# B's product of each scan state: on VectorE in the first attention and the thought, on GpSimd in the second attention's loop

## The chip, the core and the metric

The kernel runs on one core of a Trainium2 chip. The metric is the device time of one launch in microseconds (us); lower is better. A core has TensorE (PE), VectorE (DVE), ScalarE (ACT), GpSimd (POOL) and SyncE (SP), which here only issues DMAs. Each engine works through its own list of instructions in order and waits for the others by semaphores.

## What is computed

A decoder of four layers of three parts each runs on a stream x of 4 x 256 tokens with 256 features; each part adds its output to x and normalizes. The parts that matter are the first three and the next two: an attention with 16 heads (`L0_attn`), a selective scan whose output gates x (`L0_xattn`), a gated block with four recurrent "thought" steps (`L0_ffn`), a second attention (`L1_attn`) and a second selective scan (`L1_xattn`). Both scans read only the context, not x, so each can be computed any time before its gate. The scan, cut to its core:

```python
delta = softplus(dt_proj_w @ dt_lo + dt_proj_b)     # per channel and token
A = -exp(A_log)                                      # 16 states per channel
def step(state, xs):
    d_t, B_t, C_t, u_t = xs
    dA = exp(d_t[..., None] * A)
    state = state * dA + (d_t * u_t)[..., None] * B_t[:, None, :]
    y_t = einsum('ben,bn->be', state, C_t)
    return state, y_t
y = (y + D * u) * silu(z)                            # z is the stream x
```

There are 256 channels, 16 states, 4 batch elements and 256 tokens.

## The kernel before

One program does all twelve parts. Activations stay in on-chip memory; weights are loaded one part ahead. All arithmetic named below is in float32.

**The scans.** Class `Scans` (lines 398 to 531) makes both scans. Its generator `_steps` first makes u, delta and du = delta * u for all tokens (lines 446 to 487), and writes the rows of B and C to DRAM. Then come 4 x 16 = 64 "states", one for each batch element and state number. One state, on tiles of 128 partitions x 512 (two channel halves x 256 tokens), is:

- a DMA on SP's queue that spreads one row of B and one of C over all partitions, tile `bc` (line 513; 256 KB);
- two activations on ACT that make `dA` (line 517), in one of three buffers;
- the product `s = du * B` (line 519), by `K.ptt`, that is on GpSimd. This is "B's product" of the title;
- the scan along time on VectorE, in place in `s` (line 520);
- the product `s = s * C` on VectorE (line 528, by `K.tt`);
- two states later, a matmul with the identity on TensorE that adds `s` into a PSUM bank, tile `ssmps` (line 499, function `add`).

Pools `bc` and `s` have four buffers each (line 403). So a state's DMA waits for the C product of four states before, and B's product waits for the DMA and for TensorE's sum of four states before, whose buffer `s` it overwrites.

**Beside what the states run.** `K.scans.beside(n)` (line 432) takes the next n states out of the generator. The first scan's 64 states go beside the first attention, two for each of its 32 iterations (`run_mqa`, line 378). The second scan's first 24 go into the thought in one burst (`run_thought`, line 748), 8 into the preparation of the second attention (`run_gqa`, line 1030), and 32 into its loop (line 1034).

**An iteration of the first attention** (lines 368 to 384) has, on VectorE: the maxima of the scores (`nm`, line 311), the query product and the two rotated halves from PSUM (`qT`, `ropet`, lines 259 to 261, each reading one operand from PSUM), the reciprocals (`sm`, line 320). GpSimd adds the rotated halves (`qT<-qT,ropet`, line 262, both operands in on-chip memory). ACT makes the exponentials `p`, their scaling, and copies `pT` and `oT` out of PSUM. TensorE makes scores `sc`, transposes, sums `o`, the output projection `acc` and the next queries `ps`. Every eighth iteration ends a batch element: x is updated and normalized twice (`x<-x,mv,rstd`, line 164), with a GpSimd power for `rstd` in the middle (lines 166 to 170), and `gate_pair` (line 534) multiplies the gate on GpSimd.

**A thought step** (lines 708 to 739) is a chain: `rstd` on VectorE and its power on GpSimd, `tT` on VectorE, matmuls, Gelu on ACT, transposes, matmuls, and back to the next step's variance.

The order of the instructions in each engine's list is set by a scheduler when the program is built. It starts from the order of the code above and its own estimates of cost, and the list is then fixed. Helpers have one line each: `K.tt` is line 111 (VectorE), `K.ptt` line 123 (GpSimd), `K.mm` line 132 (TensorE), `K.act` line 126 (ACT).

Of the kernel before, what the change touches and what calls it, by code (L numbers as in the profile page):

```python
# [29 lines left out]
ADD, SUB, MUL, MAX, MIN = ALU.add, ALU.subtract, ALU.mult, ALU.max, ALU.min  # L30

P = 128
B, L, D = 4, 256, 256
NT = B * L // P
DC = D // P
# [5 lines left out]
class Core:  # L41


    def __init__(self, tc, ctx, A, out, first, last):
        self.tc, self.nc, self.A, self.out, self.first, self.last = tc, tc.nc, A, out, first, last
        nc = tc.nc
        const = ctx.enter_context(tc.tile_pool(name="const", bufs=1))
        self.state = ctx.enter_context(tc.tile_pool(name="state", bufs=1))
        self.x = self.state.tile([P, NT, D], F32, name="x")
        self.xT = self.state.tile([P, DC, B * L], F32, name="xT")  # L50

        self.ctxp = self.state.tile([P, B, L + 3], F32, name="ctxp")
        nc.gpsimd.memset(self.ctxp[:, :, 0:3], 0.0)
        xT = A["xT"].rearrange("(c p) t -> p c t", p=P)
        for h in range(2):
            nc.sync.dma_start(out=self.xT[:, :, 512 * h : 512 * h + 512], in_=xT[:, :, 512 * h : 512 * h + 512])

        self.idz = const.tile([P, 2 * P], F32, name="idz")
        nc.gpsimd.memset(self.idz, 0.0)
        make_identity(nc, self.idz[:, 0:P])  # L60
        self.ident = self.idz[:, 0:P]

        self.identb = const.tile([P, P], BF16, name="identb")
        nc.vector.tensor_copy(self.identb, self.ident)
        self.fin = ctx.enter_context(tc.tile_pool(name="fin", bufs=3))
        self.mean = const.tile([P, 3], F32, name="mean")
        self.power = const.tile([P, 2], F32, name="power")
        nc.gpsimd.memset(self.power, -0.5)
        self.ones = const.tile([P, P], F32, name="ones")
        nc.gpsimd.memset(self.ones, 1.0)  # L70
        self.eps = {}
        for v in (1e-6, 1.0):
            self.eps[v] = const.tile([P, 1], F32, name=f"eps{len(self.eps)}")
            nc.gpsimd.memset(self.eps[v], v)
        self._turn = 0
# [130 lines left out]
def again(ap, n):  # L206

    return ap.unsqueeze(1).to_broadcast([ap.shape[0], n, ap.shape[1]])
# [189 lines left out]
class Scans:  # L398
    def __init__(self, K, ctx):
        tc = K.tc  # L400
        self.K = K
        self.one = ctx.enter_context(tc.tile_pool(name="ssm1", bufs=1))
        self.wk = ctx.enter_context(tc.tile_pool(name="ssm2", bufs=4))
        self.ps = ctx.enter_context(tc.tile_pool(name="ssmp", bufs=1, space=PSUM))
        self.dram = ctx.enter_context(tc.tile_pool(name="ssmd", bufs=2, space=bass.MemoryType.DRAM))

        self.dA = [self.one.tile([P, DC, L], F32, name=f"dA{k}") for k in range(3)]
        for t in self.dA:
            K.nc.gpsimd.memset(t[:, :, 0:1], 0.0)
        self.w = {}  # L410
        self.left = iter(())
        self.done = 0

    def load(self, pre):
        K = self.K
# [26 lines left out]
    def _steps(self, pre):  # L442
        K, nc, w, wk = self.K, self.K.nc, self.w[pre], self.wk
        cols = w["cols"]
        N = B * L
        u = self.one.tile([P, DC, N], F32, name="u", bufs=2)
        delta = self.one.tile([P, DC, N], F32, name="delta")
        du = self.one.tile([P, DC, N], F32, name="du")


        taps = []
        for j in range(4):
            t = wk.tile([P, D], F32, name="tap", tag="bc", padded_shape=[P, 2 * L])
            nc.sync.dma_start(out=t, in_=K.A[f"{pre}_cw"][:, j * D : (j + 1) * D].to_broadcast([P, D]))
            K.ptt(t, t, w["in"], MUL)
            taps.append(t)
        for h in range(2):
            for c in range(DC):
                ps = self.bank()
                for j in range(4):  # L460
                    K.mm(ps, taps[j][:, c * P : (c + 1) * P], K.ctxp[:, 2 * h : 2 * h + 2, j : j + L], j == 0, j == 3)
                K.act(u[:, c, 512 * h : 512 * h + 512], ps, AF.Identity, bias=cols[:, c, 0:1])
        K.act(u, u, AF.Silu)
        negA = self.one.tile([P, DC, 16], F32, name="negA")
        K.act(negA, cols[:, :, 2:18], AF.Exp)
        K.ts(negA, negA, -1.0, None, MUL)
        bc = self.dram.tile([2, 16, N], F32, name="bcd")
        for h in range(2):
            s = slice(512 * h, 512 * h + 512)
            xd = wk.tile([P, 512], F32, name="xd", tag="s")  # L470
            ps = self.bank()
            for c in range(DC):
                K.mm(ps[0:40, :], w["xp"][:, c, :], u[:, c, s], c == 0, c == DC - 1)
            nc.scalar.copy(xd[0:40, :], ps[0:40, :])
            for k in range(2):
                nc.sync.dma_start(out=bc[k, :, s], in_=xd[8 + 16 * k : 24 + 16 * k, :])
            for c in range(DC):
                ps = self.bank()
                K.mm(ps, w["dt"][:, c * P : (c + 1) * P], xd[0:8, :])

                K.ts(delta[:, c, s], ps, cols[:, c, 1:2], None, ADD)
                K.act(du[:, c, s], ps, AF.Abs, bias=cols[:, c, 1:2])
        K.act(du, du, AF.Exp, scale=-1.0)
        K.act(du, du, AF.Ln, bias=K.eps[1.0])
        for c in range(DC):
            K.stt(delta[:, c, :], delta[:, c, :], 0.0, du[:, c, :], MAX, ADD)
            K.ptt(du[:, c, :], delta[:, c, :], u[:, c, :], MUL)

        turn = 0
        self.y = u  # L490

        late = []
        bank = {}

        def add(b, n, s):
            if n == 0:
                bank[b] = self.bank()
            y = bank[b]
            K.mm(y, K.ident, s.rearrange("p c l -> p (c l)"), n == 0, n == 15)
            if n == 15:  # L500
                for c in range(DC):
                    v = u[:, c, b * L : (b + 1) * L]
                    K.stt(v, v, cols[:, c, 18:19], y[:, c * L : (c + 1) * L], MUL, ADD)
                self.done += 1

        for b in range(B):
            lo = b * L
            for n in range(16):
                yield
                if len(late) > 1:  # L510
                    add(*late.pop(0))
                t = wk.tile([P, 2, L], F32, name="bc", tag="bc")
                nc.sync.dma_start(out=t, in_=bc[:, n, lo : lo + L].unsqueeze(0).to_broadcast([P, 2, L]))
                dA = self.dA[turn % 3]
                turn += 1
                for c in range(DC):
                    K.act(dA[:, c, 1:L], delta[:, c, lo + 1 : lo + L], AF.Exp, scale=negA[:, c, n : n + 1])
                s = wk.tile([P, DC, L], F32, name="s")
                K.ptt(s, du[:, :, lo : lo + L], again(t[:, 0, :], DC), MUL)
                nc.vector.tensor_tensor_scan(  # L520
                    out=s.rearrange("p c l -> p (c l)"),
                    data0=dA.rearrange("p c l -> p (c l)"),
                    data1=s.rearrange("p c l -> p (c l)"),
                    initial=0.0,
                    op0=MUL,
                    op1=ADD,
                )
                K.tt(s, s, again(t[:, 1, :], DC), MUL)
                late.append((b, n, s))
        for t in late:  # L530
            add(*t)


def gate_pair(K, pool, y, b):

    K.scans.upto(b)
    gate = pool.tile([P, DC, L], F32, name="gate")

    K.act(gate, K.x[:, 2 * b : 2 * b + 2, :], AF.Silu)
    K.ptt(gate, gate, y[:, :, b * L : (b + 1) * L], MUL)  # L540
    for t in range(2):
        ps = K.tp.tile([P, 512], F32, name="ps", tag="tp")
        for c in range(DC):
            K.nc.tensor.transpose(ps[:, c * P : (c + 1) * P], gate[:, c, t * P : (t + 1) * P], K.ident)
        K.add_out(2 * b + t, ps[:, 0:D])
# [436 lines left out]
def run_gqa(K, w, more):  # L982
    nc, tc = K.nc, K.tc
    more()
    with ExitStack() as ctx:
# [22 lines left out]
        for i in range(NT):  # L1008
# [6 lines left out]
            t = [wk.tile([P, 20, 8], F32, name=f"t{k}") for k in range(4)]  # L1015
# [15 lines left out]
        early.close()  # L1031
        if K.fused(3):
            heads16.then = lambda b: gate_pair(K, wk, K.scans.y, b)
        heads16.run(ctx, lambda: K.scans.beside(1))


# [1401 lines left out]
```

## Time and profile before

| | |
|---|---|
| runs shown | 2521.07, 2504.77, 2520.05 us; median 2520.05 |
| the profiled execution | 2505.99 us; span 2504.2 us, so 1.8 us lie around the span |
| granted TensorE clock, mean | 0.939 of full speed |
| busy: PE, DVE, ACT, POOL | 2277.2, 1460.8, 802.4, 530.6 us |
| first scan of a state begins, 64th ends | 88.6 us, 382.8 us |
| the thought's 24 states | 467.4 to 540 us |
| the preparation's 8 states | 565 to 612 us |
| the loop's 32 states | 612 to 773 us |

In the profile each group of instructions has the line that issued it, the engine, the operation, out<-in with the tiles' names, shapes and the count; behind the bar come the busy time in us, the mean of one in ns, and the engine's idle time just before these instructions with what ended it. In the timeline each row has the start and the time taken, both in us; "x2" after a row says that two alike followed each other and were merged.

### The profile page before, as it was taken

How to read it: one execution, taken by the hardware profiler on the slowest of the kernel's cores; microseconds unless marked ns; L12 is line 12 of the kernel's file. 1: busy time of each engine (PE TensorE's matmuls, PEld its weight loads, DVE VectorE, ACT ScalarE, POOL GpSimd, SP SyncE). 2: the span in 40 equal slices, each digit the busy share in tenths (PEclk: the TensorE clock that was granted, in tenths of full speed). 3: DMA queues.
4: the chain of work that ended last, by engine and by line, in shares of the span. 5: the costliest groups of instructions: out<-in, count | busy, mean ns of one | idle time of the engine just before them, and what ended most of it. 6: DMA issues, size and time to landing. Idle time of an engine off the chain costs nothing. (4 is left out here: it accounts for less than half of the span.)

```text
span 2504.2 us, 28859 instructions
## 1 busy us (share of the span) xinstructions
PE 2277.2 (91%) x10624; PEld 1526.3 (61%) x10624; DVE 1460.8 (58%) x2824; ACT 802.4 (32%) x1781; POOL 530.6 (21%) x617
## 2 busy tenths in 40 slices
PE   8798988648996999989999999999999989799997
PEld 5466654224443565545888888888776544476774
DVE  3798984588875412182356454444555667774556
ACT  3566663422442111153111111111122244343434
POOL 2544543663332222210001100011110002100001
PEclk9899999677987999999999999999988899999999
DMA  5221221122223254230123111211100002100000
GB/s 197 60 60 45 57 54 40 41 61 42 52 46 109 88 158 130 66 112 29 45 66 110 48 58 45 71 46 47 46 22 1 20 18 70 40 1 1 1 1 17
DMA packets 132836, 138.99 MB, mean 56 GB/s; under 512 B 13876, under 2 KB 120726, under 8 KB 130904
## 3 DMA queue, kind: packets, MB, share of 16 engines
q1 hardware_dynamic: 132696, 137.16, 19.1%
q8 instruction: 84, 1.38, 0.2%
q14 instruction: 56, 0.46, 0.1%
HBM read 134.27 MB, written 2.85 MB: 55 GB/s over the span
## 5 line engine op out<-in xcount | busy, mean ns | idle before, releaser
L132 PE MATMUL ps<-xw,xcT 128*128 128x256 f32 (+1 forms) x2304 | 519.0, 382 | 0.3 <-ACT YT L126 0.3
L132 PEld LDWEIGHTS ps<-xw,xcT 128*128 128x128 f32 x2304 | 430.7, 190 | 64.2 <-issue 1.9
L132 PE MATMUL sc<-kT,qT 32*128 32x256 f32 (+2 forms) x1024 | 240.7, 412 | 11.1 <-DVE qn L129 10.7
L520 DVE TENSOR_TENSOR_SCAN s<-dA,s 128x512 f32<-128x512 f32 x128 | 210.3, 1666 | 35.6 <-POOL s L123 35.4
L123 POOL TENSOR_TENSOR s<-du,bc 128x512 f32<-128x512 f32 x128 | 178.9, 1410 | 231.0 <-PE ssmps L132 191.1
L132 PEld LDWEIGHTS sc<-kT,qT 128*128 128x128 f32 (+1 forms) x1024 | 152.9, 206 | 92.3 <-issue 57.8
L132 PE MATMUL ssmps<-s,idz 128*128 128x512 f32 x256 | 147.1, 683 | 33.6 <-DVE s L111 33.5
L111 DVE TENSOR_TENSOR xp<-ps,xb 128x256 f32<-128x256 f32 x96 | 40.4, 421 | 227.0 <-PE ps L132 224.8
L126 ACT ACTIVATE dA<-delta,negA 128x255 f32<-128x255 f32 x256 | 117.7, 501 | 160.5 <-DVE s L520 160.3
L126 ACT ACTIVATE p<-sc,nm 128x256 f32<-128x256 f32 (+1 forms) x256 | 112.1, 445 | 109.5 <-DVE nm L129 103.7
L111 DVE TENSOR_TENSOR hT<-u,a 128x512 f32<-128x512 f32 x48 | 33.2, 691 | 186.1 <-PE u L132 186.1
L132 PE MATMUL o<-pT,vt 128*128 128x256 f32 (+1 forms) x352 | 121.1, 467 | 21.9 <-ACT pT L332 21.5
L123 POOL TENSOR_TENSOR xp<-xp,rn 128x128 f32<-128x128 f32 x96 | 35.2, 402 | 476.9 <-DVE rn L1406 476.9
L169 POOL TENSOR_SCALAR rstd<-mv 128x2 f32<-128x2 f32 x48 | 12.2, 255 | 551.3 <-DVE mv L161 541.4
L126 ACT ACTIVATE sq<-xp 128x1024 f32<-128x1024 f32 x24 | 25.4, 1057 | 314.3 <-DVE xp L111 314.2
L129 DVE TENSOR_REDUCE qn<-sc 128x2 f32<-128x480 f32 (+1 forms) x192 | 87.2, 506 | 43.6 <-PE sc L132 42.9
L129 DVE TENSOR_REDUCE nm<-sc 128x2 f32<-128x512 f32 (+1 forms) x128 | 77.2, 613 | 49.8 <-PE sc L132 49.2
L126 ACT ACTIVATE e<-sT 128x512 f32<-128x512 f32 x128 | 70.1, 591 | 108.3 <-PE sT L132 107.8
L1474 DVE TENSOR_TENSOR_SCAN dec<-xT,idz 128x256 f32<-128x256 f32 (+1 forms) x192 | 89.8, 537 | 25.0 <-DMA xT<-ad 25.0
L111 DVE TENSOR_TENSOR s<-s,bc 128x512 f32<-128x512 f32 x128 | 103.6, 829 | 1.1
L123 POOL TENSOR_TENSOR hT<-hT,sel 128x512 f32<-128x512 f32 x48 | 60.7, 1268 | 202.1 <-DVE hT L111 102.6
L132 PE MATMUL sT<-q,kT 32*128 32x256 f32 (+1 forms) x384 | 96.4, 502 | 1.7 <-ACT e L126 1.5
(503 smaller groups left out, 4067.1 us busy)
## 6 DMA issues: line engine op xcount, KB each, us to landing
bc<-bcd SPq DMA_DIRECT2D x128, 256.0 KB, 4.6
xw<-in_l2a_xw_dram SPq DMA_DIRECT2D x24, 768.0 KB, 4.9
xT<-ad SPq DMA_DIRECT2D x12, 1024.0 KB, 4.5
wj<-in_l1f_gate_dram SPq DMA_DIRECT2D x48, 128.0 KB, 2.6
wj<-in_l1f_up_dram SPq DMA_DIRECT2D x48, 128.0 KB, 3.1
wj<-in_l1f_down_dram SPq DMA_DIRECT2D x48, 128.0 KB, 3.5
sel<-cwd SPq DMA_DIRECT2D x32, 192.0 KB, 3.0
sel<-cwd SPq DMA_DIRECT2D x32, 128.0 KB, 3.5
```

Of the source, the lines that this page charges most:

```text
L111: self.nc.vector.tensor_tensor(out=out, in0=a, in1=b, op=op)
L123: self.nc.gpsimd.tensor_tensor(out=out, in0=a, in1=b, op=op)
L126: self.nc.scalar.activation(out, in_, func, **kw)
L129: self.nc.vector.tensor_reduce(out=out, in_=in_, axis=AX.X, op=op, **kw)
L132: self.nc.tensor.matmul(out, lhsT=lhsT, rhs=rhs, start=start, stop=stop)
L169: self.nc.gpsimd.tensor_scalar(out=out, in0=in_, scalar1=add, scalar2=None, op0=ADD)
L520: nc.vector.tensor_tensor_scan(out=s.rearrange("p c l -> p (c l)"), data0=dA.rearrange("p c l -> p (c l)"), data1=s.rearrange("p c l -> p ...
L1474: nc.vector.tensor_tensor_scan(out=dec[:, k, h, :], data0=ap[:, h, at(bb, k, j) : at(bb, k, 2)], data1=K.idz[:, 0 : (2 - j) * P], initial=0.0,
```

## The change

B's product is issued on VectorE (`K.tt`) unless a flag `apart` is set. The flag starts as false and is set when the preparation of the second attention is over, ahead of its loop. So the 64 states of the first attention, 24 of the thought and 8 of the preparation get B's product on VectorE, and the 32 of the loop keep it on GpSimd. Nothing else is edited.

```diff
@@ class Scans, __init__
         self.done = 0
+        self.apart = False
@@ Scans._steps
-                K.ptt(s, du[:, :, lo : lo + L], again(t[:, 0, :], DC), MUL)
+                (K.ptt if self.apart else K.tt)(s, du[:, :, lo : lo + L], again(t[:, 0, :], DC), MUL)
@@ run_gqa
             heads16.then = lambda b: gate_pair(K, wk, K.scans.y, b)
+        K.scans.apart = True
         heads16.run(ctx, lambda: K.scans.beside(1))
```

In the lists of the changed program, the typical iteration of the first attention reads on VectorE: two maxima, `qT`, two `ropet`, the reciprocals, two B products, two scans, two C products. SP's list is the same as before, and all lists agree again from the first states of the second attention's loop on. In the burst of the thought, each B product stands one state ahead of the scan that uses it.

## The prediction

> **What bounds the kernel now.** I read the page's busy digits first: where do the scans lie (slices of 62.6 us, so the first 13), and who is full there?
>
> ```profile
> PE   8798988648996999989999999999999989799997
> DVE  3798984588875412182356454444555667774556
> POOL 2544543663332222210001100011110002100001
> PEclk9899999677987999999999999999988899999999
> ```
>
> VectorE is at 8 to 9 tenths in slices 2 to 5 and 8 to 10 but far from it later. Only there can the change matter; behind 775 us VectorE is busy for 883 of 1729 us, and the lists are unchanged. Next, the stretches (columns after the length: PE, PEld, DVE, ACT, POOL busy, clock, DMA share, GB/s): first attention, thought, preparation.
>
> ```profile
> 84.60:385.00 300.40, 260.50 (x1070) 178.06 (x1070) 264.00 (x338) 186.74 (x532) 152.23 (x109) 0.94 0.23 55
> 465.00:540.50 75.50, 47.39 (x200) 20.86 (x201) 67.31 (x64) 32.45 (x65) 48.85 (x32) 0.82 0.35 77
> 565.00:612.00 47.00, 39.80 (x155) 22.12 (x156) 41.89 (x86) 12.44 (x35) 20.67 (x39) 0.83 0.22 45
> ```
>
> VectorE is the fullest engine in all three (88, 89 and 89%); in the first attention PE is level with it (87%). In its steady part PE is even the tighter one: over the two iterations from 214.67 to 232.37 PE is busy 17.70 of 17.70 us, VectorE 16.33. But what is in VectorE's busy time? Groups of 84.6 to 385 us:
>
> ```profile
> L520 DVE TENSOR_TENSOR_SCAN s<-dA,s 128x512 f32<-128x512 f32 x64 | 116.7, 1857 | 10.7 <-POOL s L123 10.5
> L111 DVE TENSOR_TENSOR s<-s,bc 128x512 f32<-128x512 f32 x64 | 49.1, 798 | 0.2
> L117 DVE TENSOR_SCALAR x<-x,mv,rstd 128x256 f32<-128x256 f32 x12 | 12.0, 1041 | 5.0 <-POOL rstd L123 5.0
> L123 POOL TENSOR_TENSOR s<-du,bc 128x512 f32<-128x512 f32 x64 | 85.4, 1353 | 99.5 <-PE ssmps L132 87.3 <-DMA bc<-bcd 8.6 <-PE ps L330 3.4
> L123 POOL TENSOR_TENSOR qT<-qT,ropet 128x512 f32<-128x512 f32 x24 | 49.7, 2070 | 15.6 <-DVE ropet L111 15.6
> ```
>
> The scan's mean is 1857 ns where the view of tile s gives a minimum of 1185 (median over all 128: 1226); the C product's 798 against 657. The timeline shows why:
>
> ```profile
> 218.04 2.51 POOL L123 TENSOR_TENSOR s<-du,bc 128x512 f32<-128x512 f32 x2 [4.38 <-PE ssmps L132]
> 219.36 4.42 DVE L520 TENSOR_TENSOR_SCAN s<-dA,s 128x512 f32<-128x512 f32 x2
> 220.50 2.20 POOL L123 TENSOR_TENSOR qT<-qT,ropet 128x512 f32<-128x512 f32 x1
> 227.65 1.39 DVE L111 TENSOR_TENSOR ropet<-ps,w_l0a_rope 64x512 f32<-64x512 f32 x2
> 229.07 3.38 DVE L520 TENSOR_TENSOR_SCAN s<-dA,s 128x512 f32<-128x512 f32 x2
> 229.12 2.25 POOL L123 TENSOR_TENSOR qT<-qT,ropet 128x512 f32<-128x512 f32 x1 [0.98 <-DVE ropet L111]
> ```
>
> Two scans with nothing against them take 2.33 us (568.25 in the timeline). At 229 they take 3.38: the query add on GpSimd waits for the first, and then the second waits for the add. At 219 they take 4.42: a B product blocks one and the add blocks the other. A PSUM reader such as ropet, beside the B product of 218, keeps its 0.69 each.
>
> **What the skill says.** The Trainium skill, "SBUF — State Buffer", section "Who interferes with whom", says that a VectorE instruction with two SBUF inputs contends with a GpSimd instruction that reads SBUF, and that whoever starts first holds the shared port while the other blocks entirely. The trace agrees: 1.05 us for one such meeting, none for PSUM readers. "GPSIMD Engine Reference", section "3.1 Elementwise — side-by-side cycle accounting", has GpSimd at about twice VectorE's time for a two-input product; here 1.26 us free (tile s: minimum 1257 ns) against 0.66.
>
> **The change, part by part.** A B product on VectorE is priced by the nearest row: the C product has the same shape, kinds and broadcast, 0.657 us at least, 0.63 each in unobstructed pairs (1.26 at 223.71). I take 0.65.
>
> *First attention, 64 states.*
> 1. Added: 64 x 0.65 = +41.6 us of VectorE work.
> 2. Removed: stalls behind GpSimd. Scans (1857 - 1200) x 64 = 42.0; C products (798 - 660) x 64 = 8.8; x<-x (1041 - 410) x 12 = 7.6; together 58.4. Of these the adds and the gates (24 + 1 + 3 in this stretch) hold 28 x 1.0 = 28, which stay. B products held the other 30: -30.
> 3. The adds now meet a B product, scan or C product every time, because behind ropet stand only a 0.17 us reciprocal and then six such instructions. An add of 1.26 us holds one of them for up to 1.15 instead of 1.0: 28 x 0.15 = +4. Bounds: 0, if the add finds a gap; +28 x 0.26 = 7 if it always holds a full 1.26.
> 4. Waits of VectorE: the 10.5 us for GpSimd's B product go, but the first one needs du, ready at 87.2: -7.9. Rstd's power is no longer queued behind products: -1.5 of 5.0. Waits of 6.2 for ACT's p and 10.6 for PE's ps and sc are slack of an engine ahead of PE; as VectorE becomes the last, two thirds of these 16.8 go: -11. New: B products wait on VectorE for a landing or for PE's sum of four states before: +3, an estimate (bounds under the rivals).
> Sum 41.6 - 30 + 4 - 20.4 + 3 = -2.
> Cross-check: a steady pair of iterations has 16.33 + 4 x 0.65 - 1.05 + 0.3 = 18.2 of VectorE against PE's 17.70, so +0.5 on some 8 pairs = +4; the burst of eight states at the start took 22.5 us (88.57 to 111.04), and in the new order needs 8 x 2.43 = 19.4 with one blocked add, -2; at the three batch ends the x<-x stalls and the rstd wait go, about -1.5 each. Also about -2.
>
> *Thought, 24 states.* In its stretch the scan's mean is 1811 and the C product's 992 ns: (1811 - 1200 + 992 - 660) x 24 = 22.6 us of stalls, and 5.1 us of waits for GpSimd's product. All of these go, -27.7; added 24 x 0.65 = +15.6; GpSimd's powers and gate sums now meet the products, +3; and GpSimd waited 20.8 us here for bc to land (4.6 us each), which VectorE could now do itself: a state takes 2.5 us, a buffer comes round after some 6.3 us of VectorE work against 5.1 for issue and landing, so mostly hidden; I put +4 for this and for PE's sums queued behind the step's chain. Sum -5; without that cover -1, with all of it hidden -9. The chain of a step itself, from rstd to rstd, is 8 to 9 us by its rows against a step of 17.8, so it doesn't bind.
>
> *Preparation, 8 states.* Added 8 x 0.65 = 5.2. Stalls now: (1276 - 1200) x 9 + (907 - 660) x 9 = 2.9 us, part of it from the small qn adds, which stay; -2.5. Net +3 (0 to +5). GpSimd's list is freer for qn and kn, which nobody there waits long for (0.25 us).
>
> *Loop and after*: no instruction moves: 0. GpSimd's and ACT's relief is worth nothing by itself: neither ends last. DMAs: none added, SP's list is the same; a bc landing that comes late now stops VectorE, with nm and qT queued behind it, and for those PE.
>
> Total -2 - 5 + 3 = -4. The profiled execution had 2505.99 (span 2504.2 and 1.8 around it), so 2502. The runs shown lie at 2505 and at 2520, and their median is 14 above the profiled one: 2520 - 4 = 2516.
>
> **The rivals.**
> *GpSimd gets out of the way altogether.* If the query adds, too, fall beside PSUM readers, the 28 us of stalls in step 2 and the 4 of step 3 go as well, and PE's 20.6 us of waits for pT in this stretch shrink with them: 2516 - 32 = 2484. For: GpSimd's queue is short and the add could start at once. Against: behind ropet come six two-input instructions, and PE's 17.70 a pair leaves only 0.5.
> *VectorE inherits GpSimd's waits (slower).* GpSimd stood 87.3 us, 20 times, for PE's sum of an old state; standing there cost nothing. On VectorE the same wait holds up nm and qT. Place: the B products behind the reciprocals. In the timeline PE's two sums end at 217.9 and 218.8, the products are due at 219.4 and later: cover of 1.5 us at most and 0.6 at least. If the sums slip so that each of 30 iterations loses 1.1 us, +33 - 4 = +29: 2549. It decides above 1% from about 1 us an iteration. Against: the sums depend on C products 9 us older, and a PE that is no longer last comes early.
> *Nothing comes through.* PE stays the bound in the first attention and the thought's savings turn into waits for bc and for the chain: 0 + 0 + 3 = +3, 2523. For: PE's full window above. Against: VectorE's 89%.
>
> **How the numbers follow.** Forecast 0.53, nothing comes through 0.22, waits inherited 0.13, out of the way 0.12. About 1% (25 us) is what a measurement of this kernel can tell from no change. The forecast's own range is 2505 to 2526 (-15 to +6: thought -9 to -1, first attention -8 to +6, preparation 0 to +5). The runs' own spread of 16 us adds to it, as the median may fall to the lower group; to hold 8 in 10, half of each outer rival is taken in: 2494 to 2539. Faster by over 1%: most of the first rival, 0.11. Slower: most of the second, 0.11. Within: 0.78.
>
> **What would show it.** In the changed profile: 96 B products on VectorE at 0.65 to 0.7 where free, the blocked ones near 1.8; scans in the first attention back at 1.2 to 1.3; one stall an iteration, on a B product beside the query add; a pair of iterations of 18.2 us with PE below full; the thought's 24 states 5 us shorter, the preparation 3 longer; the rest equal. Wrong would be: B products waiting for ssmps or bc by tens of us, adds without stalls, or a steady pair still at 17.7 or above 19.

## The result, and the profile after

The changed kernel takes 2471.24 us (median of 6 runs, 2464.71 to 2486.38) where the kernel before, run on the same chip, takes 2514.95: a ratio over the runs of both of 0.985, 95% interval 0.982 to 0.987 (the quotient of the two medians is 0.983, inside it). It is faster by 1.5%, where the forecast had 2516 and a range from 2494 to 2539. The profiled execution of it took 2469.83 us, its span is 2468.1.

The page of the changed kernel, busy tenths in 40 slices (61.7 us each):

```profile
PE   8889998659986999899999999999999988899997
...
DVE  3799983788875211280455444444556677774566
...
POOL 2221214132330322200011000100210002100001
PEclk9999997778887999999999999999988899999999
```

GpSimd is down to 1 and 2 tenths in the first attention (slices 2 to 6), and VectorE is at 8 and 9 in slices 3 to 6. TensorE's granted clock is 9 tenths in all five, and 7 to 8 in the thought and the preparation behind them. Where the 36.1 us of span came from is read off the scans, which both kernels have 128 of:

| from, to | before, us | after, us | difference | forecast |
|---|---|---|---|---|
| start of the span to the first scan | 88.6 | 86.5 | -2.1 | 0 |
| first attention: first scan to the end of the 64th | 294.3 | 276.7 | -17.6 | -2 |
| end of the 64th to the 65th | 84.5 | 83.6 | -0.9 | 0 |
| thought and its gates: 65th to 89th scan | 97.6 | 86.9 | -10.7 | -5 |
| preparation: 89th to 97th, with the loop's first four, to 101st | 45.3 + 27.5 | 51.9 + 16.3 | -4.6 | +3 |
| rest of the loop, 101st to the end of the 128th | 134.9 | 134.9 | 0.0 | 0 |
| behind it | 1731.6 | 1731.2 | -0.4 | 0 |

All three parts came out better than the sums, the third with the other sign. The experiments below contain stages with unchanged lists, which show how far one execution can be trusted: the first attention takes 294.3 to 296.7 us in the three executions with the lists of before and 274.9 to 276.7 in the four with those of the changed kernel; the thought takes 97.5 to 98.5 us in five and 85.3 to 86.9 in seven. The third part is less certain, as told under "The preparation". The stretches of the changed kernel (same columns as in the prediction):

```profile
83.00:364.00 281.00, 251.67 (x1067) 173.48 (x1068) 269.22 (x402) 185.37 (x531) 54.89 (x43) 0.98 0.23 58
444.70:507.50 62.80, 45.79 (x196) 18.66 (x196) 57.57 (x84) 31.43 (x64) 4.77 (x4) 0.84 0.42 92
533.70:585.70 52.00, 48.43 (x188) 27.55 (x190) 45.13 (x95) 13.26 (x35) 16.76 (x35) 0.86 0.16 37
```

In the first attention VectorE is now busy for 269.2 of 281.0 us. Its busy time rose by only 5.2 us, with 64 more instructions, and its waits for other engines fell from 33.1 to 10.8 us, summed over the groups. The groups of 83 to 364 us of the changed kernel, those that answer to the ones shown of before:

```profile
L521 DVE TENSOR_TENSOR_SCAN s<-dA,s 128x512 f32<-128x512 f32 x64 | 80.3, 1281 | 0.1
L111 DVE TENSOR_TENSOR s<-du,bc 128x512 f32<-128x512 f32 x64 | 61.6, 993 | 3.6 <-POOL du L123 3.2 <-PE ssmps L132 0.2
...
L111 DVE TENSOR_TENSOR s<-s,bc 128x512 f32<-128x512 f32 x64 | 41.7, 676 | 0.4
...
L123 POOL TENSOR_TENSOR qT<-qT,ropet 128x512 f32<-128x512 f32 x24 | 40.1, 1671 | 152.9 <-DVE ropet L111 91.6 <-PE ps L330 33.6 <-PE o L132 12.7
```

The scan fell from 1857 to 1281 ns and the C product from 798 to 676, as forecast. B's product has a mean of 993 ns, and hardly anything but du at the very start keeps it waiting: 0.2 us for TensorE's old sums (87.3 us when GpSimd stood there), none for a landing of bc. In the timeline of VectorE, the first pair, then one iteration of the steady part and the start of the next:

```profile
85.27 1.29 DVE L111 TENSOR_TENSOR s<-du,bc 128x512 f32<-128x512 f32 x2 [3.24 <-POOL du L123]
...
199.17 0.18 DVE L320 RECIPROCAL sm<-sm 128x4 f32<-128x4 f32 x1
199.27 2.33 DVE L111 TENSOR_TENSOR s<-du,bc 128x512 f32<-128x512 f32 x2
201.53 2.33 DVE L521 TENSOR_TENSOR_SCAN s<-dA,s 128x512 f32<-128x512 f32 x2
203.78 1.26 DVE L111 TENSOR_TENSOR s<-s,bc 128x512 f32<-128x512 f32 x2
...
208.34 0.18 DVE L320 RECIPROCAL sm<-sm 128x4 f32<-128x4 f32 x1
208.44 2.34 DVE L111 TENSOR_TENSOR s<-du,bc 128x512 f32<-128x512 f32 x2
```

The forecast's "one stall an iteration, on a B product beside the query add" is here: two products take 2.33 us where a free pair takes 1.29, and the scans behind them 2.33 as when free. Such a meeting costs 1.0 us. There are 25 of them in the stretch, 21 on a B product and four on a scan. The pair of iterations, from reciprocal to reciprocal, lasts 17.74 us, before 17.68.

A steady pair still at 17.7 is one of the signs of being wrong that the forecast named. The exchange on VectorE is of the kind forecast, but the 18 us lie elsewhere; the same division by reciprocals shows where (iterations counted from 0; 4 begins ahead of the first scan). The last three columns are experiments told below.

| iterations | before | after | product left out | addition left out | addition on VectorE |
|---|---|---|---|---|---|
| 4 to 8, the start | 76.9 | 74.5 | 66.0 | 72.0 | 72.7 |
| 9 to 12, first batch end | 47.4 | 40.8 | 37.9 | 37.2 | 38.9 |
| 13 to 16, steady | 36.2 | 36.3 | 35.8 | 35.6 | 36.7 |
| 17 to 20, second batch end | 43.2 | 41.4 | 38.4 | 38.5 | 39.6 |
| 21 to 24, steady | 36.1 | 36.3 | 35.8 | 35.8 | 36.7 |
| 25 to 28, third batch end | 46.0 | 41.7 | 37.7 | 37.5 | 38.8 |
| 29 and 30, the last | 17.8 | 14.4 | 14.1 | 14.5 | 13.5 |
| sum | 303.7 | 285.4 | 265.7 | 271.0 | 276.9 |

The steady iterations didn't change; the three batch ends gave 12.7 of the 18.3 us, the last two iterations 3.3, the start 2.4. The timeline of the first batch end shows the chain there. Before:

```profile
160.78 2.55 POOL L123 TENSOR_TENSOR s<-du,bc 128x512 f32<-128x512 f32 x2
160.84 2.63 DVE L117 TENSOR_SCALAR x<-x,mv,rstd 128x256 f32<-128x256 f32 x2 [0.84 <-POOL rstd L123]
...
163.51 0.63 ACT L126 ACTIVATE gate<-x 128x512 f32<-128x512 f32 x1 [1.06 <-DVE x L117]
...
164.16 1.28 ACT L126 ACT_TABLE_LOAD   x1
...
165.87 1.05 ACT L332 COPY pT<-ps 128x512 f32<-128x512 f32 x2
...
166.48 3.78 PE L132 MATMUL o<-pT,vt 128*128 128x512 f32 x4 [3.35 <-ACT pT L332]
...
166.81 4.35 DVE L520 TENSOR_TENSOR_SCAN s<-dA,s 128x512 f32<-128x512 f32 x2
```

And after:

```profile
154.48 0.73 DVE L117 TENSOR_SCALAR x<-x,mv,rstd 128x256 f32<-128x256 f32 x2 [0.84 <-POOL rstd L123]
...
156.10 0.63 ACT L126 ACTIVATE gate<-x 128x512 f32<-128x512 f32 x1
...
158.45 1.05 ACT L332 COPY pT<-ps 128x512 f32<-128x512 f32 x2
...
158.97 2.29 DVE L521 TENSOR_TENSOR_SCAN s<-dA,s 128x512 f32<-128x512 f32 x1
...
159.07 1.98 PE L132 MATMUL o<-pT,vt 128*128 128x512 f32 x4 [1.95 <-ACT pT L332]
```

Before, the two B products whose turn came with rstd's power hold `x<-x` for 1.9 us; ACT's gate waits for x and the copies of pT stand behind it on ACT's list; TensorE waits 3.35 us for pT, and its next four matmuls then take twice as long (3.78 against 1.98 us), since its granted clock halved while it stood. The adds and the gate on GpSimd then block both scans. After, `x<-x` is free, pT comes after a wait of 1.95, and TensorE keeps its clock. The two waits for rstd itself are equal, 0.84 us.

### The profile page after: what moved, and what is told of

The parts are those of the page before. It is cut to its first block, busy times and chain, and to the rows that moved or that the text cites. A ratio compares the mean times of both kernels' runs of the same rounds, so it can differ in the third digit from the quotient of the medians.

```text
span 2468.1 us, 28762 instructions
## 1 busy us (share of the span) xinstructions
PE 2265.7 (92%) x10624; PEld 1521.6 (62%) x10624; DVE 1457.9 (59%) x2920; ACT 801.0 (32%) x1781; POOL 383.2 (16%) x521
## 5 line engine op out<-in xcount | busy, mean ns | idle before, releaser
L521 DVE TENSOR_TENSOR_SCAN s<-dA,s 128x512 f32<-128x512 f32 x128 | 160.2, 1266 | 15.4 <-POOL s L123 15.3
L132 PE MATMUL o<-pT,vt 128*128 128x256 f32 (+1 forms) x352 | 115.0, 449 | 15.5 <-ACT pT L332 15.1
L129 DVE TENSOR_REDUCE qn<-sc 128x2 f32<-128x480 f32 (+1 forms) x192 | 87.1, 506 | 40.1 <-PE sc L132 38.4
L126 ACT ACTIVATE a<-g 128x512 f32<-128x512 f32 x48 | 28.7, 597 | 206.9 <-PE g L132 206.8
L132 PE MATMUL g<-xT,wj 128*128 128x512 f32 x192 | 92.1, 603 | 0.7 <-ACT rows L100 0.7
```

Of the source, the lines that this page charges most:

```text
L126: self.nc.scalar.activation(out, in_, func, **kw)
L129: self.nc.vector.tensor_reduce(out=out, in_=in_, axis=AX.X, op=op, **kw)
L132: self.nc.tensor.matmul(out, lhsT=lhsT, rhs=rhs, start=start, stop=stop)
L521: nc.vector.tensor_tensor_scan(out=s.rearrange("p c l -> p (c l)"), data0=dA.rearrange("p c l -> p (c l)"), data1=s.rearrange("p c l -> p ...
```

## The experiments

Times by stage of the runs told below, each from its profiled execution, in us; behind them the median, and the ratio of the runs to those of the kernel before on the same chip, with the 95% interval. The chips differ (medians of the kernel before from 2510.0 to 2518.3), so two experiments are compared by their ratios or by stage, not by their medians. "Preparation" is that with the loop's first four states.

| run | first attention | thought | preparation | loop | behind | median | ratio |
|---|---|---|---|---|---|---|---|
| first attention alone | 276.2 | 97.9 | 74.8 | 135.4 | 1731.2 | 2490.1 | 0.991 (0.988 to 0.993) |
| thought alone | 294.5 | 87.6 | 72.6 | 135.4 | 1731.6 | 2498.3 | 0.993 (0.991 to 0.996) |
| without the preparation | 274.9 | 87.6 | 72.7 | 135.2 | 1731.7 | 2472.4 | 0.984 (0.981 to 0.987) |
| loop too | 276.1 | 85.9 | 69.2 | 135.9 | 1732.4 | 2467.3 | 0.981 (0.978 to 0.984) |
| product left out | 259.3 | 86.8 | 72.7 | 134.0 | 1727.5 | 2447.7 | 0.972 (0.968 to 0.977) |
| batch ends alone | 284.8 | 97.5 | 75.2 | 135.4 | 1728.2 | 2509.5 | 0.998 (0.996 to 1.000) |
| addition left out | 257.5 | 86.3 | 68.7 | 135.1 | 1745.0 | 2458.3 | 0.976 (0.970 to 0.981) |
| matmuls added at the ends | 292.9 | 98.5 | 74.9 | 135.4 | 1745.1 | 2513.6 | 1.001 (0.999 to 1.003) |
| addition on VectorE | 268.6 | 85.9 | 72.7 | 134.0 | 1738.1 | 2473.4 | 0.984 (0.980 to 0.988) |
| the same, loop too | 268.4 | 85.3 | 69.6 | 137.3 | 1726.6 | 2464.6 | 0.981 (0.977 to 0.985) |
| matmuls added in the preparation | 296.7 | 97.7 | 71.3 | 136.4 | 1731.7 | 2505.6 | 0.998 (0.996 to 1.001) |
| addition, loop and matmuls | 268.6 | 86.2 | 71.8 | 136.5 | 1730.8 | 2464.5 | 0.980 (0.976 to 0.983) |

The part behind the loop has the same lists in all, but for a few instructions at its start where the loop was changed, and still spreads over 18 us. By and large it goes with the time that TensorE's clock spends halved there (95 us in the run of 1726.6, 113 in the changed kernel's 1731.2, 127 at 1738.1, 154 and 158 in the two of 1745), though not in every run (117 us at 1728.2 and at 1731.7). Runs of one kernel differ in the same way: of the kernel before on one chip, the quickest took 2500.2 us at a mean clock of 0.942, the slowest 2522.8 at 0.932. So what follows is read by stage.

**The change in parts.** The line of B's product with another condition; here and below, (...) stands for the arguments as they were:

```diff
-                (K.ptt if self.apart else K.tt)(s, du[:, :, lo : lo + L], again(t[:, 0, :], DC), MUL)
+                (K.tt if pre == "l0x" else K.ptt)(...)                          # first attention alone
+                (K.tt if pre == "l1x" and 16 * b + n < 24 else K.ptt)(...)      # thought alone
+                (K.tt if (pre == "l0x" or 16 * b + n < 24) else K.ptt)(...)     # without the preparation
+                (K.tt if True else K.ptt)(...)                                  # loop too
```

> B's product on VectorE in the first attention alone; thought, preparation and loop keep it on GpSimd. Theory V (VectorE's own time and stalls set the stretches where it is last, and TensorE's clock[...] follows): the gain of each stage is its own, so the first attention takes 275 to 279 us from first to 64th scan (before 294.3, after 276.7), the thought with its gates about 97 as before, and the whole is 18 to 21 us faster than before. Theory C (the half-clock stretches fell well for the changed kernel by chance): the first attention comes out anywhere from 280 to 294, and not with the changed kernel's three half-clock stretches. The forecast's own sum: 2 us faster.

Measured: 276.2 us in the first attention and 97.9 in the thought. The stage's gain is its own. Theory C falls: this run's TensorE spent 17.1 us at half clock there, the changed kernel's 10.2 and the kernel before's 37.5, and two further runs with 17.1 us took 274.9 and 276.1. The total, some 25 us below before where 18 to 21 were expected, has the other stages' scatter in it.

> B's product on VectorE in the thought's 24 states alone. Theory V: first attention as before, 294 +- 2 us; thought to the 89th scan 86 to 88 us (before 97.6); preparation and the loop's first four states as before, 45 and 27; the whole 10 to 12 faster. Theory O (the gain of the thought came from the changed order that the first attention's end hands to it): 93 us or more. The forecast's own sum: 5 us faster.

Measured: 87.6 us against 97.6, with everything around it as before. Theory V holds and theory O falls. The total is some 17 us below before where 10 to 12 were expected: again more than the stage.

> B's product on VectorE in the first attention and the thought, on GpSimd in the preparation and the loop: the change without its third part. Theory V with the preparation's part real: preparation plus the loop's first four states take 72 to 73 us as before, where the changed kernel took 68.2, and the whole is 3 to 6 us slower than the changed kernel. Theory P (the preparation's part costs VectorE's added 3 us, and what came back behind it is the phase of TensorE's clock): those stages take 65 to 70, and the whole is as fast as the changed kernel or up to 3 us faster.

Measured: 72.7 us, as before, so the preparation's part does bring 4.5 us in the two profiled executions, and theory P's size falls; but the ratios of the whole, 0.984 and 0.985, can't tell the two kernels apart. More on this below.

> B's product on VectorE in the loop of the second attention too, so in all 128 states. Theory V: there TensorE is busy 124 of 135 us and VectorE 109; VectorE takes over 32 x 0.65 = 20.8 us, and loses its 14.9 us of waits for GpSimd's product and 5.4 of stalls, so the loop takes 133 to 138 us against 134.9, and the whole is within 3 us of the changed kernel. Theory H (what counts is that GpSimd's products hold VectorE's port): the loop gets faster as the first attention did, by 6% or 8 us. Everything ahead of the loop as in the changed kernel.

Measured: 135.9 us. In this loop VectorE's busy time goes from 108.9 to 121.3 us and the stage's length by 1.0: TensorE, busy for 126 of these us, can hide the rest. Theory V holds: there it hardly matters which engine makes the product.

**What a product costs on either engine.** B's product left out of the first attention:

```diff
-                (K.ptt if self.apart else K.tt)(s, du[:, :, lo : lo + L], again(t[:, 0, :], DC), MUL)
+                if pre == "l0x":
+                    v = du.rearrange("p c l -> p (c l)")[:, lo : lo + 2 * L]
+                else:
+                    (K.ptt if self.apart else K.tt)(s, du[:, :, lo : lo + L], again(t[:, 0, :], DC), MUL)
+                    v = s.rearrange("p c l -> p (c l)")
-                    data1=s.rearrange("p c l -> p (c l)"),
+                    data1=v,
```

> The changed kernel with B's product left out of the first attention's 64 states (the scan reads du in its place), so neither GpSimd nor VectorE spends time on it there. It splits the change: against the changed kernel it is the price of 64 products on VectorE, against the kernel before the price of the same products on GpSimd. Theory V (VectorE's time counts only at the start burst and the batch ends; in between TensorE is full): first attention 268 to 274 us (changed kernel 276.7, before 294.3), that is 3 to 9 us for the 41.6 us of VectorE work that the forecast added. Rival (VectorE's time counts all along): 276.7 - 41.6 = 235, held at some 250 by TensorE's own work.

Measured: 259.3 us, 17.4 below the changed kernel and 35.0 below before; both theories missed the size, V by a factor of two. The stretch of this run and its scan:

```profile
85.30:344.60 259.30, 242.28 (x1062) 171.03 (x1062) 232.80 (x337) 182.69 (x529) 63.06 (x43) 0.99 0.25 63
```

```profile
L525 DVE TENSOR_TENSOR_SCAN s<-dA,du 128x512 f32<-128x512 f32 x64 | 99.5, 1591 | 2.0 <-POOL du L123 0.9 <-PE ssmps L132 0.8
```

The query add now blocks the scan (1591 ns), so the run takes away the products and leaves those stalls. A product costs 35.0/64 = 0.55 us of the stage on GpSimd and 17.4/64 = 0.27 on VectorE; the change is the difference. The second figure is less clean than the first. The scheduler also gave the changed kernel another order: some 44 of VectorE's older instructions stand elsewhere in its list than before, while this run keeps the order of before but for some four. So the 35.0 compare like orders, and the 17.4 and the change itself contain what the new order is worth. No run has the old order with the product on VectorE in all 64 states. By the table of iterations none of it is in the steady part (35.8 us without the product, 36.2 and 36.3 with it). At the batch ends it costs 9.5, 4.8 and 8.3 us on GpSimd and 2.9, 3.0 and 4.0 on VectorE; at the start 10.9 and 8.5.

**Where it matters.** The kernel before with only the 18 products around the batch ends on VectorE:

```diff
-                K.ptt(s, du[:, :, lo : lo + L], again(t[:, 0, :], DC), MUL)
+                (K.tt if pre == "l0x" and 16 * b + n in (18, 19, 20, 21, 22, 23, 34, 35, 36, 37, 38, 39, 50, 51, 52, 53, 54, 55) else K.ptt)(...)
```

> The kernel before, with only the 18 products of states 18 to 23, 34 to 39 and 50 to 55 on VectorE, that is those of the iterations around the first three batch ends. Theory V (the gain lies at the batch ends, where x<-x is behind GpSimd's products and TensorE stands until pT comes): first attention 280 to 283 us, 11 to 14 us below before, for 28% of the moved products. Rival (the gain is spread evenly over the states): 18/64 of 17.6 = 5, so 289.

Measured: 284.8 us, 9.5 below before; by iterations -5.9, -0.5 and -2.8 at the three ends. The gain is just under the range of theory V and twice the rival's 5: 28% of the products bring 54% of it. This is read by stage; over its 20 runs the whole is only 0.2% faster (0.996 to 1.000), and the profiled execution, of 2496.2 us, is the fastest of them.

**Is it TensorE's clock?** The Trainium skill, "TensorE: Matmul & The Clock Gate", section "What's actually happening", says that the clock is gated to half after a window of 3413 ns in which TensorE was idle, and that the window runs freely. The records agree in length: the half-clock stretches are 3.41, 6.83, 10.24 and 13.65 us long and so on. But the windows ahead of them are not all idle: each of the seven in the first attention of before follows 3.41 us in which TensorE was busy for 0 to 1.2. So the waits at the batch ends might cost twice. Four matmuls were put into them:

```diff
             o = po.tile([P, 512], F32, name="o")
+            for _ in range(4 if n % 8 == 0 and n else 0):
+                K.mm(o, K.ident, w["q"][:, 0, 0:512], True, True)
```

> The kernel before with four more matmuls, whose sums nothing reads, ahead of TensorE's wait for pT at each of the three batch ends (12 in all, 0.86 us each at full clock): TensorE is busy in the window in which it stood, and VectorE's, ACT's and GpSimd's lists stay as they are. Theory H (each wait of TensorE there costs a second time, by the half-clock stretch that follows it): the stretches of 6.8, 3.4 and 6.8 us behind the batch ends go, and the first attention takes 286 to 290 us against 294.3. Rival (the half clock is a symptom, and VectorE sets the pace there): 294 +- 1.5, or up to 4 longer where the added matmuls stand in the way.

Measured: 292.9 us, 1.4 below before, and -2.1, +0.5 and -0.2 at the three ends. TensorE's list was as meant, but VectorE's and ACT's were not left as they were: some C products and maxima changed places with `x<-x`, so the run isn't the clean one that its expectation says. At the second and third end a half-clock stretch of 3.41 us stayed. At the first end, though, it had what theory H asks for:

```profile
166.34 1.98 PE L132 MATMUL o<-pT,vt 128*128 128x512 f32 x4 [0.75 <-ACT pT L332]
```

```profile
165.29 3.62 DVE L522 TENSOR_TENSOR_SCAN s<-dA,s 128x512 f32<-128x512 f32 x2
```

Full clock and a wait of 0.75 us, and the end is 2.1 us shorter where the change made it 6.6 shorter. The scans are still blocked (3.62 against 2.33). So theory H explains at most a third of that end, and the half clock looks mostly like a symptom of VectorE's stalls. With the changed order and the 3.4 us of added matmuls in the run, this is argued more than shown. Runs with the same lists speak for it: 37.5 and 41.0 us at half clock went with 294.3 and 296.7 us, 10.2 and 17.1 us with 276.7 and 274.9 to 276.2.

**What the stalls that are left are worth.** The addition in `rotated` left out in one run, and made by VectorE in another:

```diff
-            K.ptt(out, out, t, ADD)          # addition left out
-            K.ptt(out, out, t, ADD)          # addition on VectorE
+            K.tt(out, out, t, ADD)
```

> The changed kernel with the addition of the rotated halves of queries and keys left out in the first attention, so that GpSimd holds VectorE's port nowhere there: the 26 us of stalls still left are gone. Theory V: most of them stand where TensorE is full, so the first attention takes 271 to 275 us, 2 to 6 below the changed kernel. The rival of the forecast (GpSimd gets out of the way altogether, stalls count in full): 250 us.

Measured: 257.5 us by the scans (of which some is a shorter lead-in), 14.4 us less by the iterations; more than theory V's 2 to 6, less than the rival's 27. Again the steady iterations gain only 0.5 to 0.7.

> The changed kernel with the addition of the rotated halves (32 of queries, 2 of keys) on VectorE too, so that no GpSimd instruction of the first attention's loop but the gates reads two operands beside VectorE. Theory V, with the prices of the two runs that leave work out: with no addition at all the first attention took 257.5 us, and 64 products on VectorE cost 17.4 us, 0.27 each, so 34 additions cost 9: 264 to 270 us against 276.7. Rival (an addition on VectorE costs what its stall cost, because VectorE's busy time is what it was: 34 x 0.65 = 22 added against 26 of stalls): 273 to 277.

Measured: 268.6 us: theory V. The stalls are gone and VectorE is busy for 257.5 of 268.5 us, 10 less than the changed kernel's 267.3 of 276.7, although the additions are now its own. The ratio of the whole, 0.984, is yet that of the changed kernel: preparation and the part behind the loop, whose lists are unchanged, took 4.5 and 7 us longer.

> The same, and B's product on VectorE in the loop of the second attention too. Theory V: as with the additions alone up to the loop (first attention 264 to 270), and the loop within 2 us of 135, so 7 to 13 us faster than the changed kernel. Rival: no difference to the changed kernel.

Measured: 2464.6 us; the first attention as expected and 137.3 in the loop, 0.3 above the range. The ratios to the kernel before, 0.981 (0.977 to 0.985) here and 0.985 (0.982 to 0.987) for the changed kernel, do not tell the two apart; on their own chips they lie 45 and 44 us below before.

**The preparation.** Why did its part win where VectorE had more to do? Its six profiled executions with GpSimd's product took 72.6 to 75.2 us, and those with VectorE's 68.2, 68.7, 69.2, 69.6, 72.7 and 72.7, the last two (product left out, addition on VectorE) with the changed kernel's lists in this stage. First the whole stretch and then the half-clock part in it, before:

```profile
565.00:637.80 72.80, 65.07 (x262) 34.62 (x262) 57.41 (x108) 19.32 (x48) 25.88 (x43) 0.74 0.19 40
```

```profile
609.30:633.20 23.90, 23.23 (x69) 11.41 (x67) 14.07 (x20) 5.45 (x12) 2.52 (x2) 0.50 0.18 39
```

The changed kernel:

```profile
533.70:602.00 68.30, 64.22 (x262) 35.44 (x262) 58.17 (x113) 19.52 (x48) 19.45 (x37) 0.81 0.18 43
```

```profile
583.77:597.42 13.65, 13.14 (x40) 7.12 (x36) 10.98 (x16) 4.87 (x10) 0.00 (x0) 0.50 0.30 78
```

And with the addition on VectorE, same lists in this stage as the changed kernel:

```profile
526.00:598.60 72.60, 69.67 (x246) 38.22 (x250) 57.96 (x112) 19.42 (x48) 19.21 (x37) 0.71 0.21 44
```

```profile
568.98:599.70 30.72, 30.21 (x106) 16.65 (x109) 22.36 (x33) 8.82 (x18) 6.41 (x6) 0.50 0.21 52
```

TensorE is busy nearly all the time in the half-clock parts, VectorE is not. The stage's length goes with the clock and not with VectorE's work, in all twelve executions just named: with 26 to 32 us of half clock in the stage it takes 68.2 to 69.6 us (four, all with VectorE's product), with 38 us 72.6 to 72.8 (three, GpSimd's), with 42 us 72.7 (two, VectorE's), with 44 us 74.8 to 75.2 (three, GpSimd's). A run in which TensorE gets more to do tests that:

```diff
                     scs = [self.ps.tile([P, 2, L], F32, name="sc") for _ in rs]
+                    if self.kinds == [(0, L)] and 6 <= self.begun < 15:
+                        K.mm(scs[0], K.ident, K.ctxp[:, 0:2, 3 : 3 + L])
```

> The kernel before with nine more matmuls of 128 rows x 512, whose sums nothing reads, between the maxima's 32-row matmuls at the end of the preparation and the start of the loop (9 x 0.86 = 7.7 us of TensorE work at full clock). It asks why the preparation's part won 4 us where the forecast had lost 3: preparation and the loop's first four states took 72.7 us with GpSimd's product and 68.2 with VectorE's, with the same TensorE work, but a half-clock stretch of 23.9 us against 13.7. Theory H (TensorE's half clock sets the pace there, and 32-row matmuls do not end it): the stretch behind 609 us shrinks to under 12 us, and the two stages take 66 to 73 us although TensorE has more to do. Rival (VectorE or the chain sets the pace, the clock follows): 75 to 81 us.

Measured: 71.3 us with nine more matmuls, against 72.7. The stretches:

```profile
608.86:615.69 6.83, 6.83 (x15) 2.70 (x15) 3.00 (x6) 1.11 (x3) 0.78 (x1) 0.50 0.32 65
615.69:632.76 17.07, 17.07 (x83) 8.49 (x82) 12.24 (x18) 4.33 (x9) 3.01 (x3) 1.00 0.17 28
```

The half clock ends after 6.83 us, where all six executions with GpSimd's product and without these matmuls have a stretch of 23.9, and 7.7 us of added work cost less than nothing. Theory H holds: with GpSimd's product, TensorE's clock sets the pace in this stage. The median, 2505.6 against 2510.0 of before on the same chip, is not told apart from it.

> A candidate for a version that beats both: additions and all products on VectorE (2464.6 us), and five more 128 x 512 matmuls, whose sums nothing reads, between the 32-row matmuls at the end of the preparation (5 x 0.86 = 4.3 us). Theory H (the half clock sets the pace there): preparation and the loop's first four states take 66 to 70 us (69.6 without the five), the half-clock stretch is under 10 us, and the whole comes to 2458 to 2465. Rival (with VectorE's products there the half clock no longer matters): 72 to 75 us for the two stages, and 2467 to 2470.

Measured: 71.8 us in the preparation, between the two theories' ranges; the 2464.5 us of the whole are within theory H's, but the version without the five matmuls took the same. The last half-clock stretch was shorter than without them (10.2 us against 20.5), and the stage was 2.2 us longer, so in this version the clock alone doesn't set the length. With the addition on VectorE the first attention took 268.4 to 268.6 us in all three versions, 6 to 8 below the changed kernel's lists; the best ratio of a version that leaves nothing out is 0.980 (0.976 to 0.983), which is not told apart from the changed kernel's.

## Why the prediction was wrong

*What bounds the kernel now*: right. The gain lies in the three stages that were named, and no instruction moved behind the loop's first states.

*First attention*, "Sum 41.6 - 30 + 4 - 20.4 + 3 = -2" against -17.6: the step that failed. Its two groups of terms, against VectorE's own account of the stretch: the added and removed work came to +5.2 us of busy time where the sum has +15.6, and the waits to -22.3 where it has -17.4. Term by term:
- added work and stalls on it (step 1 and the adds' 32 of steps 2 and 3): 61.6 us by the group, forecast 73.6. The adds hold 21 products for 20.6 us and four scans for 4.3, not 28 instructions for 32, and the gates hold nothing. Rows of the timeline also overlap their neighbours by some 0.07 us, so 64 more rows cost some 5 us less of busy time than their durations add up to (an estimate, 64 x 0.07).
- removed stalls: scans 116.7 to 80.3 and C products 49.1 to 41.7, 43.8 us where the forecast had 50.8; 4.4 of the 7 are the adds still on the scan, as (1281 - 1213) x 64: it takes 1213 ns with the additions on VectorE. The 7.6 us of `x<-x` all went (12.0 to 4.4).
- "New: B products wait on VectorE for a landing or for PE's sum": 0.2 us, forecast 3. The waits for p, ps and sc fell from 16.9 to 2.6 us, where two thirds were forecast. Rstd kept 4.8 of its 5.0, where 1.5 were to go.

The larger fault is not in a single term. The sum adds microseconds of VectorE from places where they are worth different amounts. The run without the product shows it: 64 products on VectorE cost 17.4 us, not 48.6, because in the steady iterations they cost next to nothing; on GpSimd they cost 35.0, of the 50.4 that steps 2 and 4 credit. Two errors of 31 and 15 us, with opposite signs, left 16; that they offset each other by half is luck. (What the new order of the list adds to this is not separated, as told above.) The cross-check was by place, and would have found it, had its ends been worked out: "a steady pair ... 18.2" was 17.74, so not +4 but about 0; "at the three batch ends the x<-x stalls and the rstd wait go, about -1.5 each" were -6.6, -1.8 and -4.3. It left out the eight states of each end, whose blocked scans and products are on the path there, and the chain from `x<-x` over ACT to TensorE's wait. The last two iterations (-3.3), where no more queries are made, were not looked at.

*Thought*, -5 against -10.7 (-10.0 alone): the mechanism as forecast. The two terms that were set against it, +3 for meetings with GpSimd's powers and gates and +4 for landings and TensorE's sums, came to 1 or 2 together (-27.7 + 15.6 = -12.1 without them), past the forecast's own end of -9. The groups of 465 to 540.5 us of before:

```profile
L520 DVE TENSOR_TENSOR_SCAN s<-dA,s 128x512 f32<-128x512 f32 x24 | 42.9, 1811 | 5.1 <-POOL s L123 5.1
L111 DVE TENSOR_TENSOR s<-s,bc 128x512 f32<-128x512 f32 x24 | 23.4, 992 | 0.2
```

And of 444.7 to 507.5 us of the changed kernel:

```profile
L521 DVE TENSOR_TENSOR_SCAN s<-dA,s 128x512 f32<-128x512 f32 x24 | 29.0, 1217 | 0.0
L111 DVE TENSOR_TENSOR s<-du,bc 128x512 f32<-128x512 f32 x24 | 15.8, 675 | 4.5 <-POOL du L123 4.5
L111 DVE TENSOR_TENSOR s<-s,bc 128x512 f32<-128x512 f32 x23 | 15.6, 684 | 0.1
```

Scans, B products and C products run at their free durations, and only du, ahead of the first state, is waited for.

*Preparation*, +3 against -4.6: the step priced VectorE, and TensorE at half clock sets the pace. How much of the 4.6 is the change and how much the length of the half-clock stretches, which differs between executions with the same lists, stays open: of six executions with VectorE's product two gained nothing.

*Loop and after*, 0: right, but that the part behind the loop came out within 0.4 us of before is luck, as the same lists spread over 18 us there. The base of the forecast was 5 us off as well: the median of 2520 us of three runs was 2515 in the six beside the changed kernel.

*The rivals.* "GpSimd gets out of the way altogether" gave 2484, the nearest time, by a mechanism that didn't happen: the adds still block 21 products and four scans. "VectorE inherits GpSimd's waits" cost 0.2 us. "Nothing comes through" holds for the steady iterations and for nothing else.

## What to carry to other kernels

Where two engines take turns as the last one, don't net added and removed work of an engine over a whole stage: cut the stage where the bound changes, and price each side of the change in each piece; here a product cost 0.55 us on GpSimd and 0.27 on VectorE on the mean, and next to nothing on either in the steady part. At the seams look at what the blocked instruction hands on: 1.9 us on two `x<-x` of 0.4 us went over ACT's list to TensorE. In the preparation, where TensorE was busy at half clock, its granted clock told more of the stage's length than VectorE's account; look at both.

## What was not expected of the hardware

TensorE's clock halved, and stayed halved, while TensorE was busy: 23.23 of 23.90 us in the preparation of before, and 2.47 of the 3.41 us ahead of it. The idle window of the page cited above doesn't cover this. Most of its matmuls there (52 of 67) read 32 rows; nine matmuls of 128 rows among them cut the stretch to 6.83 us. That it is the rows that count is argued, not shown.

Identical lists gave stretches of 13.65 us in one execution and 30.72 in another. Behind the loop, lists that agree but for a few instructions had 95 to 158 us of half clock and took 1726.6 to 1745.1 us.
